# The wait for ScalarE's queue ahead of the centring of the expert weights, and the planner's margin for landings

## The chip, the cores and the metric

The kernel runs on one core of a Trainium2 chip (trn2). The metric is the device time of one execution in microseconds, lower is better; three executions of the kernel before gave 3122.73, 3131.1 and 3135.55 us, the median being 3131.1 us. Profiles come from one profiled execution of their own.

## The reference

Eight images of 256 channels and 32 by 32 pixels pass through two layers, all in float32.

- Layer 0: a group norm, then attention with 8 heads of 32 channels. Queries are a 1x1 product of the normed image. Keys and values come from another 1x1 product, averaged to four sizes (32, 16, 11 and 5 pixels a side, 1426 places in all), each with a depthwise 3x3 convolution added, then normed over channels. The heads' outputs are mixed by a small softmax matrix, projected and added to the image.
- Layer 1: the image is read as tokens. A layer norm and a single-head attention of size 256 over the image's 1024 tokens of 256 channels, added; a second layer norm, and a mixture of 8 experts, added.

The experts are what the change's weights belong to:

```python
feat = jnp.mean(x, axis=0)
w = jax.nn.softmax(feat @ Wr + br, axis=-1)
h = jnp.einsum('bfd,edh->bfeh', x, W1) + b1
h = jax.nn.relu(_bn(h, g1, be1, m1, v1))
h = jnp.einsum('bfeh,ehk->bfek', h, W2) + b2
h = jax.nn.relu(_bn(h, g2, be2, m2, v2))
y = jnp.einsum('bfeh,ehd->bfed', h, Wo) + bo
return jnp.einsum('bfed,fe->bfd', y, w)
```

The layer norm ahead of the experts subtracts the mean over channels. The kernel does that once in the weights instead of in each token: it multiplies each expert's W1 (and the router's Wr) by the matrix I - 1/256, which it calls `cm`, and stores the product as `w1c`.

## The kernel before

**Stages.** `attention` (L955) does layer 0 of all images and, beside it, layer 1 of the images that are through. `experts` (L2350) follows. A check at the end may send the program into a general version, which this data doesn't take.

**The main loop** (L2161 to L2206) runs over steps: for each image, each half of the channels (4 heads), each half of the pixels and 11 groups of up to 128 keys, plus one step per image for the last 25 keys of all halves: 45 steps an image, 360 in all. A step issues `scores` (L1651): four products of 32 x 512 into the one PSUM tile `sc`, and ScalarE's exponential of it into a tile `pt`; then `values` (L1661) of the step before, from `pt` into `pv`. Pairs of `pt` are added by GpSimd's accumulating DMA (`add`, L1706). As `sc` has one buffer, the scores of a step wait for the exponential of the one before.

**Threads.** All else is written as generators, each with a rank, that are spawned into a list (`spawn`, L883): keys and values of the next image, its depthwise convolutions on VectorE, pooling on GpSimd, the projection, layer 1 (`layer1`, `outputs`), and `weights1` (L1991). Each yields what it needs before its next instructions: an engine, tiles, and perhaps a PSUM tag; or a condition.

**The planner** is the class `Flow` (L666). While the program is built, every instruction issued through it is noted (`note`, L787): a cost by engine and size moves the engine's own clock `now`, and each tile gets a time at which it is ready. Each instruction is bound to follow the one issued before it on its engine, so the order in which the program is written is the order in which each engine works. After scores and after values the main loop calls `step` (L924), which resumes the first thread whose need is `runnable` (L897) until none is:

- A need of PE: a rank's credit (`PACE` and `PACE1` fill it each step), a free PSUM slot, and tiles landed, with `MARGIN`, before the time at which `sc` comes free.
- A need of another engine: if the tiles are there by that engine's clock, the engine may be ahead of TensorE by at most `AHEAD` (2.0 for ACT); else they have to land by TensorE's clock plus `NEAR`.
- `landed` (L893) is a tile's ready time, and `LATE` more if a DMA wrote it.

Where TensorE has a long planned wait and a PSUM slot is free, `warm` (L848) issues dummy products of constants.

**weights1** (L1991) runs after `mix` and ahead of `outputs` in one thread of rank 5 (L2145). It makes `cm`, the centred matrices of layer 1, and the folded batch norms; then, for each of the eight experts (L2059), loads W1 into `we` (SP's queue), yields a need of ACT with `we`, takes a second buffer of the same tag `res`, and runs `centred` (L1975): a need of PE with `src`, `cm` and a PSUM slot; four products of 128 x 256 (split in four of 32 columns each where TensorE works in that tiling); a need of ACT; ScalarE's copy to `wc`. SP stores `wc` to `w1c`. Then the router's weights follow in the same way, and `ready` lets `layer1` begin, once the first image's projection is done too.

**experts** begins when all images are projected. It loads the weights, then alternates first layers (`first7`) and second layers (`second`), while the rest of layer 1 runs as threads until `gates` has the router's weights (L2404, it needs the last image's layer 1). Up to there second layers are plain products (`half`, four of 512 columns) and their outputs go to memory; after it they use a seven-product form (`layer7`, `products`), and third layers are taken in between.

All instructions issued through the planner carry line L679 in the profile; groups are told apart by tile names.

Of the kernel before, what the change touches and what calls it, by code (L numbers as in the profile page):

```python
# [34 lines left out]
CAP = (1.5, 1.5)  # L35
NEVER = 1e9
MARGIN = 1.5
LATE = 3.0
AHEAD = {"DVE": 4.0, "ACT": 2.0, "POOL": 1.0, "SP": 10.0}
NEAR = {"DVE": 1.5, "ACT": 2.0, "POOL": 1.0, "SP": 10.0}  # L40
OWN = {"pt", "p1"}
# [624 lines left out]
class Flow:  # L666
# [226 lines left out]
    def landed(self, name):  # L893

        return self.ready.get(name, 0.0) + LATE * (self.writer.get(name) == "DMA")

# [58 lines left out]
def attention(tc, kit, f, outer, ended, nb, consts, x, t1, t2, hn, bounds, vecs, q_t, kv_t, proj_t, gqk_t, wqk, wqkv, vecs1, w1_d, w1c, gate_d, wrc, vecs2, bnvec, w2_d, h2d, between, pre, held):  # L955
# [6 lines left out]
    with ExitStack() as ctx:  # L962
# [5 lines left out]
        def T(pool, shape, tag, bufs=1):  # L968
            return f.tile(pool, shape, tag, bufs=bufs)

        def small():
            if f.also and f.free("sx") < min(map(f.end, f.slots.get("sm", [None]))):
                return T(psum, [P, 512], "sx")
            return T(shared, [P, 512], "sm", bufs=2)
# [57 lines left out]
        def rstd(out, var, eps, scale=1.0):  # L1032
            f.ve.tensor_scalar(out, var, scale, eps, ALU.mult, ALU.add)
            f.pool.tensor_tensor(out, out, kit.mhalf[: out.shape[0], 0:1].to_broadcast(out.shape), ALU.pow)
# [107 lines left out]
        def pe(*tiles, tag=None):  # L1142
            return "PE", tiles, tag

        def ve(*tiles):
            return "DVE", tiles, None

        def act(*tiles, tag=None):
            return "ACT", tiles, tag
# [825 lines left out]
        def centred(cm, src, width, dst):  # L1975

            yield pe(src, cm, tag="sm")
            ps = small()
            for m in range(2):
                for k in range(2):  # L1980
                    f.pe.matmul(
                        ps[:, m * width : (m + 1) * width],
                        lhsT=cm[:, k, m * P : (m + 1) * P],
                        rhs=src[:, k, :],
                        start=k == 0,
                        stop=k == 1,
                    )
            yield act(ps)
            f.act.activation(dst, ps[:, : 2 * width].rearrange("p (m f) -> p m f", m=2), AF.Copy)

        def weights1():  # L1991


            raw = T(l1, [P, 2, 512], "y")
            f.sp.dma_start(raw, wqk)
            wvr = T(l1, [P, 2, C], "p1", bufs=6)
            f.sp.dma_start(wvr, wqkv.rearrange("(k p) f -> p k f", p=P)[:, :, 2 * C :])
            cm = T(l1, [P, 2, C], "p1", bufs=6)
            bqkv = T(wp, [P, 6], "bqkv")
            f.sp.dma_start(bqkv, vecs1)  # L2000
            for k in range(2):
                for m in range(2):
                    f.ve.tensor_scalar(
                        cm[:, k, m * P : (m + 1) * P], ident, float(k == m), 1.0 / C, ALU.mult, ALU.subtract
                    )
            yield pe(raw, tag="sm")
            ps = small()
            for m in range(2):
                for k in range(2):
                    f.pe.matmul(  # L2010
                        ps[:, m * C : (m + 1) * C],
                        lhsT=raw[:, k, m * P : (m + 1) * P],
                        rhs=raw[:, k, C:],
                        start=k == 0,
                        stop=k == 1,
                    )
            yield ve(ps)
            g = T(l1, [P, 2, C], "p1", bufs=6)
            f.ve.tensor_copy(g, ps.rearrange("p (m f) -> p m f", m=2))
            yield from centred(cm, g, C, gw)  # L2020
            yield ve(gw)
            gm = T(wp, [P, 2], "gm")
            f.ve.tensor_reduce(gm, gw, AX.X, ALU.add)
            f.ve.tensor_scalar(gm, gm, 1.0 / C, None, ALU.mult)
            for k in range(2):
                f.ve.tensor_scalar(gw[:, k, :], gw[:, k, :], gm[:, k : k + 1], None, ALU.subtract)
            yield pe(bqkv, tag="sm")
            ps = small()
            for m in range(2):
                for k in range(2):  # L2030
                    f.pe.matmul(
                        ps[:, m : m + 1],
                        lhsT=raw[:, k, C + m * P : C + (m + 1) * P],
                        rhs=bqkv[:, k : k + 1],
                        start=k == 0,
                        stop=k == 1,
                    )
            yield ve(ps)
            u0 = T(wp, [P, 2, 1], "u0")
            f.ve.tensor_copy(u0, ps[:, 0:2].unsqueeze(2))  # L2040
            yield from centred(cm, u0, 1, gu.unsqueeze(2))
            yield from centred(cm, wvr, C, wv)
            f.ve.tensor_copy(gb, bqkv[:, 4:6])

            raw = T(l1, [P, 10, 2 * NE], "rec1")
            f.sp.dma_start(raw, vecs2)
            for i in range(2):
                b_, g_, be_, m_, v_ = (raw[:, 5 * i + u, :] for u in range(5))
                s = bnvec[:, (2 * i) * 2 * NE : (2 * i + 1) * 2 * NE]
                c = bnvec[:, (2 * i + 1) * 2 * NE : (2 * i + 2) * 2 * NE]  # L2050
                yield ve(raw)
                rstd(s, v_, 1e-3)
                yield ve(s)
                f.ve.tensor_tensor(s, s, g_, ALU.mult)
                f.ve.tensor_tensor(c, b_, m_, ALU.subtract)
                f.ve.tensor_tensor(c, c, s, ALU.mult)
                f.ve.tensor_tensor(c, c, be_, ALU.add)

            for e in range(NE):  # L2059
                we = T(l1, [P, 2, C], "res", bufs=2)  # L2060
                f.sp.dma_start(we, w1_d[:, e])
                yield act(we)
                wc = T(l1, [P, 2, C], "res", bufs=2)
                yield from centred(cm, we, C, wc)
                f.sp.dma_start(w1c[:, e], wc)
            wr = T(wp, [P, 2, NE], "wr")
            f.sp.dma_start(wr, gate_d[:, : 2 * NE].rearrange("p (k e) -> p k e", k=2))
            wrs = T(wp, [P, 2, NE], "wrs")
            yield from centred(cm, wr, NE, wrs)
            f.sp.dma_start(wrc, wrs)  # L2070
            f.drop(wvr, cm, g)
            ready.append(True)
# [70 lines left out]
        f.spawn(chain(*map(prepare, range(nb))), 4)  # L2143
        f.finish(lambda: key_parts[0] > 0)
        later.append(f.spawn(chain(mix(), weights1(), outputs()), 5))  # L2145
        f.spawn(layer1(), 6)
        aside = f.spawn(experts_ahead(), 8)
# [776 lines left out]
```

## Time and profile before

| what | us |
|---|---|
| median of three runs | 3131.1 |
| profiled execution, its own time | 3130.97 |
| its span, first to last instruction | 3128.8 |
| TensorE (PE) busy | 3034.8 |
| VectorE (DVE) busy | 2309.7 |
| ScalarE (ACT) busy | 1627.4 |
| GpSimd (POOL) busy | 1286.7 |
| TensorE's waits for ScalarE's exponential (sc <- ACT pt) | 39.3 |

The span is what the profile divides; 2.2 us lie around it. A line of a group gives engine, operation, output and inputs by tile names (numbers left out), shapes and count, and then times. Lines of waits give the total, how often, and the longest. A float32 product shows as two matmul records. The expert weights' loads run from 145.5 to 277.6 us of the span and the last store of a centred expert at 290.4 us; layer 1 begins with a load at 352.1 us, and the weights of the experts' stage are loaded from 1852.0 us on. The granted clock of TensorE is 0.993 in the mean.

### The profile page before, as it was taken

Reading aid. Unit: us, or ns where it says so; the run is one execution under the profiler, and the core shown is the slowest. Engines: PE = TensorE matmul, PEld = TensorE weight load, DVE = VectorE, ACT = ScalarE, POOL = GpSimd, SP = SyncE. Lnnn points to the kernel's source line nnn. Section 1 sums busy time; section 2 is a strip of 40 time slices with the busy share of each in tenths; the row PEclk is TensorE's granted clock in tenths of the full one; section 3 lists DMA queues with packets and bytes.
Section 4 is the critical chain, followed back from the end, with each engine's and each line's share of the span. In section 5 each row is a group of like instructions: output and inputs, shape, how many; then the busy total and the mean of one; then the engine's idle time right before and its main releaser. Section 6 shows DMA issues by size and latency. Waiting matters only on the chain.

```text
span 3128.8 us, 57003 instructions
## 1 busy us (share of the span) xinstructions
PE 3034.8 (97%) x23042; PEld 1781.0 (57%) x23042; DVE 2309.7 (74%) x3884; ACT 1627.4 (52%) x2176; POOL 1286.7 (41%) x1401
## 2 busy tenths in 40 slices
PE   7888999999999999999999999999999999999998
PEld 4323244343334343343433357778888888888887
DVE  6875988788977887788654444558888777777776
ACT  3776766666666666666655532343333344444443
POOL 3333432332242322322212120057655677777776
PEclk9999999999999999999999999999999999999999
DMA  1377766756756757656767663244443110000000
GB/s 56 83 151 169 159 134 135 167 125 132 171 108 143 173 112 148 152 125 145 171 148 156 125 204 125 105 169 143 143 152 135 46 37 25 31 21 21 21 14 22
DMA packets 113073, 360.24 MB, mean 115 GB/s; under 512 B 13776, under 2 KB 39928, under 8 KB 89344
## 3 DMA queue, kind: packets, MB, share of 16 engines
q0 software_dynamic: 28608, 181.68, 29.9%
q1 hardware_dynamic: 80688, 172.82, 16.3%
q8 instruction: 184, 3.01, 0.4%
q10 hardware_dynamic: 3504, 1.99, 0.2%
q14 instruction: 89, 0.73, 0.1%
HBM read 110.89 MB, written 78.16 MB: 60 GB/s over the span
## 4 chain that ended last, share of the span: by engine, by line
PE 74%; DVE 8%; issue 3%; ACT 2%; DMA 2%; POOL 2%; DVEq 0%; POOLq 0%; SPq 0%; ACTq 0%
PE bank L679 22%; PE sm L679 18%; PE y L679 11%; PE sc L679 8%; PE pv L679 8%; PE sx L679 7%; ACT pt L679 2%; DMA pt<-pt 1%; DVE acc L679 1%; DVE h L679 1%; DVE pt L679 1%; DVE sacc L679 1%; DVE u L679 1%; DVE c L679 1%; DMA hn<-pool 1%
## 5 line engine op out<-in xcount | busy, mean ns | idle before, releaser
L679 ACT ACTIVATE pt<-sc 128x2048 f32<-128x2048 f32 (+1 forms) x352 | 660.6, 1877 | 319.1 <-PE sc L679 238.8
L679 DVE TENSOR_TENSOR pt<-pt,pt 128x1024 f32<-128x1024 f32 x300 | 368.5, 1272 | 125.5 <-DMA pt<-pt 112.8
L679 PE MATMUL sc<-q,kn 32*128 32x512 f32 (+2 forms) x3072 | 417.0, 644 | 41.6 <-ACT pt L679 39.3
L679 PE MATMUL pv<-pt,vt 128*32 128x512 f32 (+1 forms) x2816 | 380.3, 612 | 0.0
L679 ACT ACTIVATE h<-h,bnvec 128x512 f32<-128x512 f32 x456 | 345.0, 805 | 62.6 <-DVE h L679 50.5
L679 ACT ACTIVATE p1c<-bank 128x256 f32<-128x256 f32 x228 | 87.1, 382 | 554.5 <-PE bank L679 554.3
L679 POOL TENSOR_TENSOR rstd<-rstd,mhalf 128x4 f32<-128x4 f32 (+1 forms) x96 | 116.1, 1210 | 609.4 <-DVE rstd L679 518.4
L679 DVE SCALAR_TENSOR_TENSOR acc<-map,vec,acc 128x961 f32<-128x961 f32 (+1 forms) x240 | 306.9, 1281 | 15.7 <-ACT acc L679 10.2
L679 DVE TENSOR_TENSOR h<-p1c,bank 128x512 f32<-128x512 f32 x228 | 155.2, 681 | 212.3 <-PE bank L679 209.1
L679 POOL DMA_DIRECT2D pt<-pt x160 | 147.0, 921 | 350.6 <-ACT pt L679 257.2
L679 POOL TENSOR_TENSOR tm<-h,tm 128x256 f32<-128x256 f32 x214 | 246.5, 1152 | 16.8
L679 DVE TENSOR_TENSOR h<-u,bank 128x256 f32<-128x256 f32 x456 | 232.0, 550 | 7.9
L679 PEld LDWEIGHTS sc<-q,kn 32*128 32x128 f32 (+2 forms) x3072 | 112.8, 177 | 209.0 <-ACT pt L679 93.6
L679 POOL TENSOR_TENSOR tm<-h 128x512 f32<-128x512 f32 x107 | 140.4, 1312 | 200.8 <-ACT h L679 200.8
L679 DVE SCALAR_TENSOR_TENSOR sacc<-small,vec,sacc 128x480 f32<-128x480 f32 (+8 forms) x384 | 201.7, 533 | 13.6 <-ACT sacc L679 3.6
L679 PEld LDWEIGHTS pv<-pt,vt 128*32 128x32 f32 (+1 forms) x2816 | 55.8, 108 | 271.9 <-issue 257.7
L679 DVE TENSOR_TENSOR h<-h,gate 128x1024 f32<-128x1024 f32 x128 | 203.9, 1593 | 0.5 <-ACT h L679 0.5
L679 PE MATMUL y<-t,s3e 128*128 128x256 f32 x768 | 187.0, 379 | 1.8 <-POOL t L679 1.8
L679 POOL TENSOR_TENSOR t<-h,t 128x256 f32<-128x256 f32 x220 | 175.4, 797 | 17.3
L679 POOL TENSOR_TENSOR t<-h 128x512 f32<-128x512 f32 x110 | 142.6, 1297 | 94.3 <-DVE h L679 79.9
L679 PE MATMUL bank<-t,s1e 128*128 128x256 f32 x726 | 177.2, 379 | 0.3 <-DVE h L679 0.2
L679 DVE TENSOR_TENSOR u<-h,bank 128x512 f32<-128x512 f32 x228 | 156.6, 687 | 24.2 <-PE bank L679 0.5
(369 smaller groups left out, 5619.7 us busy)
## 6 DMA issues: line engine op xcount, KB each, us to landing
pt<-pt POOLq DMA_DIRECT2D x160, 1024.0 KB, 7.8
h<-h SPq DMA_DIRECT2D x104, 512.0 KB
xi<-in_x_dram SPq DMA_DIRECT2D x16, 512.0 KB
t<-t SPq DMA_DIRECT2D x8, 1024.0 KB
res<-t SPq DMA_DIRECT2D x32, 256.0 KB
t<-res SPq DMA_DIRECT2D x32, 256.0 KB
hn<-res SPq DMA_DIRECT2D x32, 256.0 KB
hn<-hn SPq DMA_DIRECT2D x16, 512.0 KB
```

The lines of the kernel that those rows point to most:

```text
L679: ins = fn(*args, **kwargs)
```

## The change

The line that yields a need of ACT with the loaded weights is removed, so that the thread goes on at once to take the second buffer and to ask for TensorE; the load is then awaited there, as `src` in `centred`. And `LATE`, which `landed` adds to every tile written by a DMA, goes from 3.0 to 2.8, for the needs of all threads.

```diff
-LATE = 3.0
+LATE = 2.8
...
             for e in range(NE):
                 we = T(l1, [P, 2, C], "res", bufs=2)
                 f.sp.dma_start(we, w1_d[:, e])
-                yield act(we)
                 wc = T(l1, [P, 2, C], "res", bufs=2)
                 yield from centred(cm, we, C, wc)
                 f.sp.dma_start(w1c[:, e], wc)
```

No instruction of the computation is added or removed by the diff itself. As the planner's clocks depend on all that was issued before, both edits can alter the order of everything after the first load of an expert's weights.

## The prediction

> **What bounds the kernel now.** I read the page's header and slices first, then a table of stretches, then TensorE's waits, then the order in time around the change.
>
> ```profile
> span 3128.8 us, 57003 instructions
> PE 3034.8 (97%) x23042; PEld 1781.0 (57%) x23042; DVE 2309.7 (74%) x3884; ACT 1627.4 (52%) x2176; POOL 1286.7 (41%) x1401
> ```
>
> TensorE (PE) is busy in 97% of the span: 3128.8 - 3034.8 = 94 us are idle. The time is TensorE's work plus its idle time, so the question is whether the change alters either. The stretches say where the idle time lies (columns: length, then busy us of PE, its weight loads, VectorE, ScalarE, GpSimd; then granted clock, DMA share, GB/s):
>
> ```profile
> 0.00:100.00 100.00, 77.45 (x274) 38.71 (x274) 69.57 (x141) 48.08 (x88) 41.93 (x60) 0.97 0.20 60
> 100.00:420.00 320.00, 284.13 (x2463) 99.38 (x2462) 240.33 (x431) 214.09 (x260) 100.85 (x115) 0.97 0.67 146
> 420.00:1830.00 1410.00, 1394.01 (x14612) 568.62 (x14605) 1054.12 (x1913) 882.59 (x1036) 380.41 (x464) 1.00 0.66 143
> 1830.00:2040.00 210.00, 209.77 (x824) 149.45 (x823) 99.81 (x210) 65.97 (x110) 27.45 (x48) 0.99 0.40 141
> 2040.00:3129.00 1089.00, 1069.40 (x4881) 924.86 (x4879) 845.83 (x1193) 416.69 (x683) 736.10 (x715) 1.00 0.20 70
> ```
>
> Idle: 22.6 us at the start, 35.9 in the attention of image one and the start of two (100 to 420), 16.0 in the other images, 0.2 at the passage to the experts, 19.6 after it. The change acts in the second stretch; the reshuffle it sets off reaches the next two.
>
> ```profile
> PE sc L679 <- ACT pt L679: 39.3, 46, 2.6
> PE sx L679 <- DMA pt<-ptail: 2.9, 1, 2.9
> ```
>
> The largest wait is that of the scores for ScalarE's exponential of the step before; 24.8 us of it lie in 100 to 420. TensorE waited for a transfer once. How such a wait arises is seen in the order of time (start, length, what; in brackets idle time before it and its releaser):
>
> ```profile
> 274.51 1.93 PE L679 MATMUL sm<-res,p 128*32 128x256 f32 x32 [0.44 <-ACT bin L679]
> 279.52 1.14 PE L679 MATMUL sc<-q,kn 32*128 32x512 f32 x8 [1.00 <-ACT pt L679]
> 282.65 1.14 PE L679 MATMUL sc<-q,kn 32*128 32x512 f32 x8 [0.69 <-ACT pt L679]
> ```
>
> There is one score buffer, so scores, exponential and the next scores follow one another: 282.65 - 279.52 = 3.13 us at least. TensorE's own part of a step is 1.14 (scores) and 1.00 (the value products). A step into which the planner puts nothing else leaves 3.13 - 2.14 = 1.0 us idle, which is the wait shown at 279.52; one group of products (1.7 to 1.9 us) closes it. The expert weights' centring (sm<-res,p, 1.93) is such a filling.
>
> ```profile
> 180.60 0.33 SPq L679 DMA_DIRECT2D w1c<-res  x1
> 181.04 0.96 SPq L679 DMA_DIRECT2D res<-in_w_dram  x1
> 192.36 1.20 SPq L679 DMA_DIRECT2D res<-in_w_dram  x1
> ```
>
> One expert at a time: the load at 181.04 follows the store of the expert before by 0.44 us, its products run at 189.32, 8.3 us after the load. There is slack in that: eight experts take from 145.5 to 290.4.
>
> **What the Trainium skill says.** "TensorE: Matmul & The Clock Gate", the specification table at its head: ScalarE, VectorE and GpSimd take their queues strictly in order, and TensorE's reordering only pulls weight loads ahead of running matmuls. So a product helps only in the step where the planner wrote it. The trace agrees: TensorE stands for 1.00 us before scores although later products have their inputs. [...] the trace gives no landing time for the 256 KB weight loads, only the 8.3 us from load to use. "Perfetto Trace Analysis", Identifying the Most-Contended Engine: matmul busy time is no measure of nearness to the peak. I use it here only as the time that is not waiting, with the products' counts beside it.
>
> **The change, part by part.** Its size can't be read from the diff: the planner writes one order for the whole kernel, and both edits alter choices in it. I compared the orders of both builds, engine by engine, and priced them with durations of the trace. A step is one of the 360 groups of scores (45 per image); products are counted as the program issues them (the profile shows each f32 product twice).
>
> Removed wait. No instruction is removed: the eight loads, 8 x 1.9 = 15 us of products, eight copies of 0.60 us and eight stores remain. The place of the products moves. Before they follow steps 17, 20, 24, 27, 31, 37, 40 and 44, and the router's weights 47; after, 16, 22, 27, 30, 33, 39, 43, 48, and 51. So they do not come sooner: the first does, by one step, then the others spread, since the copy out of PSUM still asks for ScalarE and the product still asks for a landed load and a share of the step. That the set ends four steps later costs nothing: layer 1 needs also the first image's projection, which ends at step 57 or 58 in both orders, 6 steps (over 20 us) after. If that cover were gone, layer 1 would start some 4 x 4 us later (57 steps take about 250 us there), and other filling would be missing for that time.
>
> SP's queue. Loads and stores of weights change places with the pooled queries' stores (hn<-pool) and with an input copy (t<-in_x_dram). Each is 0.3 to 1.2 us of issue on a queue that is mostly empty, in steps whose filling doesn't read them: 0. Below nothing there is nothing to win either. If an expert's store stood waiting for its copy, the load of the next image (xi) would be behind it; in the new order that load stands ahead of the fifth store. 0, at most 2.
>
> Smaller margin. A product whose operand comes by DMA may be planned 0.2 us sooner. Were the transfer late each time, it would cost 0.2 us in each of about 100 places (8 loads of t, of xi, of the weights, the projection's inputs and products of them), 20 us; the trace shows one wait for a transfer, 2.9 us. At the other end a place taken 0.2 us sooner wins no more than a whole starved step now and then. I take 0; ends -3 and +5.
>
> The reshuffle: starved steps. For each step I sum what stands in it (scores 1.14, values 1.00, the rest by its rows; the planner's dummy products on constants left out) and take what is missing to 3.13. Before: 10.5 us in image one, 3.4 in image two, 2.8 in the six others, 16.7 in all, in 23 steps. After: 11.8, 5.5, 5.7, that is 23.0 in 27 steps. Steps with nothing at all beside scores and values rise from 12 to 23. Difference +6.3 us. The trace's waits for the exponential are 39.3 us where this sum gives 16.7, since ScalarE also has other work in front of it; in that proportion the difference would be 6.3 x 39.3 / 16.7 = 14.8. I take 6.3, as the waits of exactly 1.00 are the ones that the order decides; ends 0 and 15.
>
> The reshuffle: passage to the experts. Attention holds 1929 us of TensorE work after, 1960 before (the sums of all steps): two of the 32 layer-1 units (units 26 and 27, some 15 us each) now run among the experts' products. TensorE is full there (209.77 of 210.00), so this is moved, not saved. But the gates, which need the last image's layer 1, come later, and four more second layers run as plain products (16 of 512 columns) instead of the seven-product form (28 of 256). A plain one takes 8 x 0.465 = 3.72 us (55.8 us over 120 records), the other 3.02 (28 in 6.04 us in the chain's end), +0.70 each: +2.8 us. Twelve more intermediate tiles go out to memory and back, 24 transfers of 512 KB, where the DMA share is 0.42: 0, if that cover is gone perhaps 2. Dummy products fall from 13 units of 256 columns to 7, but they stand in idle time: 0, and in the sum above.
>
> Sum: +6.3 + 2.8 = +9 us. The profiled execution took 3130.97 us, 2.2 more than its span, and lies on the median of 3131.1. So 3131 + 9 = 3140 us, 0.3% slower, less than a measurement of this kernel tells from no change (0.5%, 15.6 us; the three runs before span 0.4%).
>
> **Rivals.** No difference (3131): the fewer dummies and starved steps trade places, because ScalarE, not the order, sets the waits; for it, that two thirds of the 39.3 us are not explained by my sum. Faster (3119): the products fill the waits of image one as the change intends. Half of its 24.8 us would be 12. Against it: of the seven steps from 29 to 45 that are empty in the old order, the weights come into just one (30), and the new order has others empty. Slower by over 0.5% (3156): each of the 11 further empty steps costs not 1.0 but up to the longest wait, 2.6 us, when the exponential stands behind copies or behind a GpSimd accumulation (pt<-pt, 7.8 us to landing) that ScalarE has to wait for; place: images one to eight; with 2.0 each it is 22 us, and with the 2.8 it gives 25. It decides from (15.6 - 2.8) / 11 = 1.2 us per empty step. That the change does nothing is excluded by the order.
>
> **Chances.** Forecast (+3 to +15) 0.45, no difference 0.27, faster 0.14, slower beyond 0.14. The range 3119 to 3156 reaches to both rivals' times; the likeliest case's own is 3134 to 3146. Faster by over 0.5% needs more than the fast rival's 12 us: 0.06. Slower by over 0.5%: 0.15. Within: 0.79.
>
> **What would show it.** Right: some 6 to 15 us more in the scores' wait for the exponential, spread over images two to eight too; 100 to 420 within 3 us of before; 144 records of 512-column products of w2e instead of 120; no new wait for a transfer. Wrong: a wait for landings of several us in TensorE's list (the margin), a shorter stretch to 420 (the fast rival), or single waits above 2 us at the empty steps (the slow one).

## The result and the profile after

The changed kernel took 3144.6 us (median of 10 runs, 3141.05 to 3149.64), the kernel before 3132.83 us in the runs beside it (10 runs). The ratio is 1.0041, 95% interval 1.0032 to 1.0049: 12.8 us slower, 10.0 to 15.4; the two medians alone differ by 11.8. The profiled execution of the changed kernel took 3145.04 us, with a span of 3143.2 us, 14.4 more than the span before.

The head of the page after:

```profile
span 3143.2 us, 56320 instructions
PE 3036.1 (97%) x22694; PEld 1782.1 (57%) x22694; DVE 2305.6 (73%) x3880; ACT 1625.5 (52%) x2172; POOL 1270.6 (40%) x1377
```

TensorE's busy time grew by 1.3 us; its idle time went from 94.0 to 107.1 us. Busy time holds the planner's dummy products too, 5.8 us before and 3.2 us after. Without them the work grew by 3.9 us (3029.0 to 3032.9) and the rest of the span by 10.5 us (99.8 to 110.3). So most of the loss is waiting. The same stretches as before, with the same columns (the first pair of numbers is the length and TensorE's busy time):

```profile
100.00:420.00 320.00, 286.54 (x2420) 99.44 (x2421) 241.25 (x437) 217.87 (x265) 99.28 (x118) 0.96 0.68 149
420.00:1830.00 1410.00, 1382.29 (x14287) 564.44 (x14286) 1047.31 (x1893) 878.00 (x1030) 389.27 (x462) 1.00 0.65 142
1830.00:2040.00 210.00, 209.31 (x820) 151.65 (x820) 98.43 (x213) 65.88 (x111) 30.56 (x50) 1.00 0.38 136
2040.00:3143.00 1103.00, 1080.78 (x4910) 928.53 (x4909) 849.68 (x1202) 417.23 (x684) 710.21 (x691) 0.99 0.24 82
```

From 100 to 420 us, where the edited code runs, idle time did not grow (33.5 us, before 35.9). It grew from 420 to 1830 us, from 16.0 to 27.7 us, long after the last expert weight was centred, and by 2.6 us after 2040. TensorE's waits after, whole execution (total, times, longest):

```profile
PE sc L679 <- ACT pt L679: 42.6, 49, 4.1
PE sx L679 <- issue: 3.5, 1, 3.5
PE sm L679 <- DMA t<-t: 2.3, 1, 2.3
```

The scores' wait for the exponential grew by 3.3 us. This total hides the wait that the prediction counted. For each wait of the scores I looked at what the exponential ahead of it had waited for. Where it had waited for its own scores alone, which is the bare chain of scores, exponential and scores, TensorE stood 20 times for 12.0 us before and 32 times for 20.7 us after. All other waits of the scores, behind ScalarE's other work, transfers or VectorE, fell from 28.4 to 22.4 us.

Two waits stand here that the kernel before did not have, and its one wait for a transfer (2.9 us for pt<-ptail) is gone. The second of the two, for the landing of an image of layer 1 (t<-t), has an entry of 2.3 us, 12 us after its transfer was issued. The first is at the passage to the experts. TensorE there (start, length, what, idle time before it):

```profile
1811.39 1.88 PE L679 MATMUL sm<-t,gw 128*128 128x512 f32 x4
1816.73 3.01 PE L679 MATMUL sx<-pt,con 128*32 128x512 f32 x8 [3.46 <-issue]
```

and VectorE, which makes the sum that this product reads:

```profile
1813.14 4.63 DVE L679 TENSOR_TENSOR pt<-pt,pt 128x1024 f32<-128x1024 f32 x4 [7.70 <-DMA pt<-pt]
```

VectorE waited 7.70 us for an accumulating transfer of GpSimd's queue, then added for 4.63 us, and the last unit's denominators could not start. The product then ran at half clock. In the order before, the same product followed without a wait of note (0.4 us idle between the last exponential and the experts' first load, against 4.1 after). TensorE had as much other work at this place in both orders: from the last value products to this sum it was busy for 5.75 us before and for 5.79 us after. What differs is the transfer. Before, with VectorE's sum, TensorE's product and the load of an image on SP's queue:

```profile
1806.72 0.86 POOL L679 DMA_DIRECT2D pt<-pt  x1 [7.80 <-ACT pt L679]
1814.30 2.36 DVE L679 TENSOR_TENSOR pt<-pt,pt 128x1024 f32<-128x1024 f32 x2 [1.78 <-DMA pt<-pt]
1818.57 2.14 PE L679 MATMUL sx<-pt,con 128*32 128x512 f32 x8
1818.77 0.43 SPq L679 DMA_DIRECT2D pt<-in_x_dram  x1
```

and after:

```profile
1800.56 0.40 SPq L679 DMA_DIRECT2D pt<-in_x_dram  x1
1800.80 0.87 POOL L679 DMA_DIRECT2D pt<-pt  x1 [6.67 <-ACT pt L679]
```

The transfer landed 7.48 us after its issue before, and 12.25 us after it in the changed kernel. There the load of 1 MB stands 0.24 us ahead of it; before, that load came 12 us behind it.

I divide each profile at the first and last exponential of the 360 steps (so that later tables can be compared). Idle time of TensorE, before and after: ahead of the steps 18.2 and 19.9; in the steps 56.0 and 60.6; to the experts' first load 0.4 and 4.1; to the gates 0.0 and 0.0; from the gates on 19.4 and 22.4. The sum of the differences is 13.0 us, beside the 1.3 us of busy time.

### The profile page after: what moved, and what is told of

Same layout as the page of the kernel before. It is cut to its first block, busy times and chain, and to the rows that moved or that the text cites. A ratio compares the mean times of both kernels' runs of the same rounds, so it can differ in the third digit from the quotient of the medians.

```text
span 3143.2 us, 56320 instructions
## 1 busy us (share of the span) xinstructions
PE 3036.1 (97%) x22694; PEld 1782.1 (57%) x22694; DVE 2305.6 (73%) x3880; ACT 1625.5 (52%) x2172; POOL 1270.6 (40%) x1377
## 3 DMA queue, kind: packets, MB, share of 16 engines
q0 software_dynamic: 28608, 181.68, 29.6%
q1 hardware_dynamic: 84144, 185.40, 17.4%
## 4 chain that ended last, share of the span: by engine, by line
PE 70%; DVE 9%; DMA 3%; issue 3%; ACT 2%; POOL 2%; DVEq 0%; POOLq 0%; ACTq 0%; SPq 0%
PE bank L679 22%; PE sm L679 16%; PE y L679 11%; PE sc L679 8%; PE pv L679 7%; PE sx L679 7%; DMA pt<-pt 2%; DVE pt L679 2%; ACT pt L679 2%; DVE acc L679 1%; DVE h L679 1%; DVE sacc L679 1%; DVE u L679 1%; DVE c L679 1%; POOL t L679 0%
## 5 line engine op out<-in xcount | busy, mean ns | idle before, releaser
L679 PE MATMUL sc<-q,kn 32*128 32x512 f32 (+2 forms) x3072 | 417.2, 644 | 43.7 <-ACT pt L679 42.6
L679 ACT ACTIVATE h<-h,bnvec 128x512 f32<-128x512 f32 x448 | 338.9, 805 | 63.8 <-DVE h L679 54.8
L679 DVE SCALAR_TENSOR_TENSOR acc<-map,vec,acc 128x961 f32<-128x961 f32 (+1 forms) x240 | 306.7, 1280 | 17.8 <-ACT acc L679 12.2
L679 POOL TENSOR_TENSOR tm<-h,tm 128x256 f32<-128x256 f32 x206 | 239.2, 1161 | 16.2
L679 PE MATMUL sm<-y,t 128*32 128x256 f32 (+1 forms) x1952 | 176.9, 380 | 1.2 <-DVE res L679 1.2
L679 POOL TENSOR_TENSOR t<-h,t 128x256 f32<-128x256 f32 x212 | 168.4, 794 | 16.6
```

What stands on the lines that cost most here:

```text
L679: ins = fn(*args, **kwargs)
```

## The experiments

All are compared with runs of the kernel before on the same chip. For each kernel with another order I counted, before it ran, the order's sum of starved steps as in the prediction; theory A is that the time follows this sum. The kernels are called e1 to e12.

**Each edit by itself.** Only the wait removed (e1):

```diff
-                yield act(we)
```

> Only the wait for ScalarE's queue is removed, the margin stays 3.0. Theory A (the time follows the order's sum of starved steps, plus 0.70 us for each second layer that runs plain instead of in seven products): the order's sum is 23.8 us against 16.4 before, and one more plain second layer (20 against 19), so 7.4 + 0.7 = +8 us, ratio about 1.0026. Rival B (the smaller margin lets TensorE reach tiles before they land, and that is what costs): no cost here, ratio 1.000, no wait for a transfer in TensorE's list. Rival C (any other order costs or wins by accidents that the sum does not see): anything within +-0.5%, not ordered by the sum over the four kernels of this set.

Measured: 3152.83 us, ratio 1.0068 (1.0049 to 1.0087). Only the margin (e2):

```diff
-LATE = 3.0
+LATE = 2.8
```

> Only the margin for landings goes to 2.8, the wait for ScalarE's queue stays. Theory A: the order's sum of starved steps is 23.3 us against 16.4, one more plain second layer, so 6.9 + 0.7 = +8 us, ratio about 1.0024, although dummies rise from 13 to 19 units. Rival B: this carries the whole loss, ratio about 1.004, with waits for transfers of 2 us and more in TensorE's list. Rival C: within +-0.5%, not ordered by the sum.

Measured: 3146.77 us, ratio 1.0047 (1.0033 to 1.0060). Theory A has the sign of both and the size of neither: it expected 8 us for each, and some 21 and 15 us were lost. Each edit alone loses more than, or as much as, both together (1.0041), so the effects of the two do not add up: each makes another order. Rival B does not hold: the removed wait alone, with the margin as before, costs most, and neither profile shows a wait for a transfer after 420 us.

**Two more orders.** The wait removed and a margin of 3.4 (e3):

```diff
-LATE = 3.0
+LATE = 3.4
...
-                yield act(we)
```

> The wait for ScalarE's queue removed, the margin larger, 3.4. Theory A: the order has fewer starved steps than before (11 empty steps, sum 14.0 against 16.4) and two more plain second layers (21 against 19), so -2.4 + 1.4 = -1 us, ratio about 1.000 (0.9985 to 1.001). Rival B: a larger margin can only take waits for landings away, of which there was one of 2.9 us: ratio 0.999 to 1.000 as well. Rival C: within +-0.5%, not ordered by the sum.

Measured: 3144.03 us, ratio 1.0038 (1.0024 to 1.0052). Theory A missed this one. The scores' wait did fall, to 31.0 us, as the sum of 14.0 says, and the idle time in the steps was that of before (56.4 us). But other waits took the place, which the sum doesn't hold: 6.3 us for VectorE's sums of pairs, 4.2 of them at the passage, where TensorE stood for 5.1 us in all; 3.8 us for the copy of a value bank; and, in spite of the larger margin, 4.2 us for loads of expert weights (res<-in_w_dram). Rival B, by which a larger margin only takes such waits away, misses here too. The wait kept and a margin of 2.7 (e4):

```diff
-LATE = 3.0
+LATE = 2.7
```

> The wait for ScalarE's queue stays, the margin is 2.7. Theory A: the sum of starved steps is 29.6 us, the largest of the orders looked at, one more plain second layer: 13.2 + 0.7 = +14 us, ratio about 1.0044. Rival B: a margin smaller still than 2.8 costs more than that one, with waits for transfers in TensorE's list. Rival C: within +-0.5%, not ordered by the sum. If A holds, the four ratios stand in the order e3, then e1 and e2, then e4.

Measured: 3168.67 us, ratio 1.0119 (1.0099 to 1.0139). The four ratios stand in the order that theory A foretold, e3, then e2 and e1, then e4, and two of them lie beyond rival C's 0.5%. The scores' wait is 60.4 us. But the loss is over twice the 14 us expected, as in e1 and nearly in e2. In e4 TensorE has no wait for a transfer of over 0.8 us, against rival B.

**A larger margin that should lose, a smaller one that should not.** Rival B is tried at its opposite ends. The wait kept and a margin of 3.05 (e5):

```diff
-LATE = 3.0
+LATE = 3.05
```

> The kernel before with a slightly larger margin for landings, 3.05 instead of 3.0; the wait for ScalarE's queue stays. Theory A (starved steps of the order): its sum is 32.9 us against 16.4, 28 empty steps against 12, one more plain second layer. The four runs so far gave 1.3 us of TensorE idle time in the steps per us of the sum, so +21 us there, and about 10 us that all of them had outside; +25 to +40 us, ratio 1.008 to 1.013. Rival B (a smaller margin costs by waits for landings, a larger one can't): ratio 1.000. Rival C (accidents of the order that the sum doesn't see): 0.998 to 1.008.

Measured: 3165.27 us, ratio 1.0103 (1.0086 to 1.0120). A margin larger by 0.05 us in the planner's reckoning costs 32 us. That is inside what was expected, but this expectation had been fitted to the four runs above, to 1.3 us of idle time in the steps for each us of the sum and 10 us besides. And the removed wait with a margin of 2.6 (e6):

```diff
-LATE = 3.0
+LATE = 2.6
...
-                yield act(we)
```

> The wait for ScalarE's queue removed, the margin 2.6, smaller than in the change. Theory A: the sum of starved steps is 16.1 us against 16.4 before, with as many plain second layers (19): 0 from these two terms; with what all four reordered kernels had outside the steps, 0 to +10 us, ratio 1.000 to 1.003, that is less than the change as made. Rival B: a margin still smaller than 2.8 costs more than the change, ratio above 1.0045. Rival C: anything within +-0.8%.

Measured: 3130.8 us, ratio 0.9995 (0.9985 to 1.0006), no loss, so the 10 us besides do not belong to every changed order. Its scores' wait, beside that of the kernel with 3.05, first this one:

```profile
PE sc L679 <- ACT pt L679: 34.3, 38, 4.2
```

then the one with 3.05:

```profile
PE sc L679 <- ACT pt L679: 48.5, 57, 3.2
```

The eight orders side by side, by the sum of starved steps:

| kernel | sum in the order, us | waits of the bare chain, us | TensorE idle in the steps, us | ratio |
|---|---|---|---|---|
| e3 | 14.0 | 9.8 | 56.4 | 1.0038 |
| e6 | 16.1 | 14.4 | 53.1 | 0.9995 |
| before | 16.4 | 12.0 | 56.0 | 1 |
| changed | 22.8 | 20.7 | 60.6 | 1.0041 |
| e2 | 23.3 | 16.3 | 62.4 | 1.0047 |
| e1 | 23.8 | 16.6 | 68.5 | 1.0068 |
| e4 | 29.6 | 20.5 | 74.7 | 1.0119 |
| e5 | 32.9 | 24.5 | 73.4 | 1.0103 |

The sums of the kernel before and of the changed one are counted anew here; the prediction had 16.7 and 23.0. A straight line through the sum and the idle time gives 1.15 us of idle time in the steps for each us of the sum, and 1.4 us where the dummies count as idle, as they do in the sum. Through the sum and the waits of the bare chain it gives 0.7 us. So the price taken per starved step, its bare 1.0 us, is near for TensorE's idle time, and neither edit has a price of its own: what they do to the order has. The time rises faster. The ratios rise with the sum, save e3, and save e5, which lies below e4 (their intervals overlap); a straight line through them gives 1.8 us of time for each us of the sum and misses e3 by 11 us. e4 and e5 lost 37 and 32 us, with 18.7 and 17.4 us more idle time in the steps.

**The dummies.** The changed kernel, its order kept (e7), with each dummy noted by the planner as before but issued with one column:

```diff
-            self.pe.matmul(t[:, :C], lhsT=self.kit.ones, rhs=self.kit.con[:, :C], start=True, stop=True)
+            ones, con = self.kit.ones, self.kit.con[:, :C]
+            cuts = range(0, P, DH) if self.narrow(ones, con) else (None,)
+            for j in cuts:
+                s = slice(None) if j is None else slice(j, j + DH)
+                ins = self.tc.nc.tensor.matmul(t[s, :1], lhsT=ones[:, s], rhs=con[:, :1], start=True, stop=True)
+                self.note("PE", "matmul", ins, (t[s, :C],), {"lhsT": ones[:, s], "rhs": con})
```

> The changed kernel with its order kept, and each planned dummy product (seven units of 256 columns in all) cut to one column, so that TensorE does nothing in these places. Theory A: the dummies stand in idle time, so the time is that of the changed kernel, ratio 1.003 to 1.005 against the kernel before. Rival: the dummies are work on the path, then 7 x 0.48 = 3 us less, ratio 1.002 to 1.004; or they keep the granted clock up, then it is slower than the changed kernel.

Measured: 3146.61 us, ratio 1.0042 (1.0026 to 1.0058), that of the changed kernel. TensorE's idle time in the steps rose from 60.6 to 67.3 us, and the time stayed. The dummies stand in idle time, as the prediction took it.

**Plain second layers.** The kernel before, 18 more of them plain (e8):

```diff
+            if i % 6 == 0:
+                tms.pop(i, None)
             if i in tms:
```

> The kernel before, its attention untouched, with 18 more of the experts' second layers as plain products of 512 columns instead of the seven-product form (37 against 19). Prediction's step: 0.70 us each, 18 x 0.70 = +12.6 us, ratio 1.0040. Rival: the plain form also spares sums on VectorE and combinations that TensorE waits for (6.8 us of waits for VectorE in that stage), so less than half of it, +0 to +6 us, ratio 1.000 to 1.002.

Measured: 3140.6 us, ratio 1.0017 (1.0007 to 1.0026), 5.3 us or 0.3 us for each (0.12 to 0.45). The prediction's 0.70 was over twice too large. From the gates on the span grew by 6.7 us (1087.5 to 1094.2) and TensorE's busy time by 6.5 us. Its idle time there stayed (19.4 and 19.5 us): the waits for VectorE's sums fell from 6.8 to 5.7 us, and others grew as much. So the rival has the size but not the cause. The price itself was mis-sized. One plain layer at full clock, seen in the changed kernel, and the product after it:

```profile
2055.76 3.60 PE L679 MATMUL bank<-h,w2e 128*128 128x512 f32 x8
2059.20 1.03 PE L679 MATMUL bank<-hn,w1e 128*128 128x256 f32 x4
```

It holds TensorE for 2059.20 - 2055.76 = 3.44 us, 0.42 us more than the 3.02 of the other form. The mean of 0.465 us, from which the prediction took 3.72, also held the time by which each group overlaps the next (3.60 shown, 3.44 to the next start) and layers at half clock, such as this one in the kernel before:

```profile
2030.79 5.38 PE L679 MATMUL bank<-h,w2e 128*128 128x512 f32 x8
```

**The kernel before again, and filled steps.** While reading the changed kernel I saw its products run at half their speed after a cluster of starved steps:

```profile
283.47 1.14 PE L679 MATMUL sc<-q,kn 32*121 32x512 f32 x8 [1.00 <-ACT pt L679]
284.53 1.06 PE L679 MATMUL pv<-pt,vt 128*32 128x512 f32 x8
288.78 2.09 PE L679 MATMUL sc<-q,kn 32*128 32x512 f32 x8 [3.18 <-ACT pt L679]
290.80 1.93 PE L679 MATMUL pv<-pt,vt 121*32 121x512 f32 x8
292.66 1.93 PE L679 MATMUL pv<-ptail,vz 32*32 32x512 f32 x8
294.52 2.09 PE L679 MATMUL sc<-q,kn 32*128 32x512 f32 x8
```

The table of stretches shows that the granted clock had fallen (it is the third last column):

```profile
285.00:290.00 5.00, 1.82 (x16) 0.51 (x8) 2.73 (x2) 1.88 (x1) 4.69 (x7) 0.79 0.84 231
290.00:295.00 5.00, 5.00 (x26) 0.88 (x24) 0.00 (x0) 2.22 (x2) 3.77 (x6) 0.50 0.95 195
```

The exponential ahead of the wait of 3.18 us was late for another reason than a starved step. It had stood for GpSimd's accumulating transfer:

```profile
286.85 1.88 ACT L679 ACTIVATE pt<-sc 121x2048 f32<-121x2048 f32 x1 [3.44 <-DMA pt<-pt]
```

Windows at half clock might still make a starved step dearer than its 1.0 us, and explain the steep rise of the ratios. So I tried a theory A': put dummies where TensorE stands, and the windows go, and time with them. First a control (e9):

> The kernel before, unchanged, as a control of what one profile says. Ratio 1.000. If the start of the profile (about 1.5 us more idle time ahead of the first step in nearly all the other kernels) and the wait at the passage belong to the run and not to the order, they are seen here too: idle time before the first step about 20 us instead of 18.2, the rest of the idle time within 3 us of the first profile. If they belong to the order, they are as in the first profile of this kernel.

Measured: 3132.48 us, ratio 1.0004 (0.9995 to 1.0014). Idle time 18.7 us ahead of the steps, 54.1 in them, 1.3 at the passage. So a profile repeats to about 2 us in a stretch, and of the 1.7 us more ahead of the steps in the changed kernel part is such scatter. Then the filled steps, in the changed kernel (e10), the kernel before (e11) and e6 (e12), each with its order otherwise unchanged:

```diff
+                placed = f.last["PE"]
                 f.step((PACE, PACE1))
+                if f.last["PE"] == placed and f.free("sm") <= f.now["PE"]:
+                    f.occupy()
...
+    def occupy(self):
+
+        bank, self.keep = self.keep, None
+        t = bank()
+        self.open.discard(t.name)
+        for j in range(0, P, DH):
+            ins = self.tc.nc.tensor.matmul(
+                t[j : j + DH, :384], lhsT=self.kit.ones[:, j : j + DH], rhs=self.kit.con[:, :384], start=True, stop=True
+            )
...
+            self.last["PE"] = ins.ins.name
+        self.keep = bank
```

> The changed kernel with its order kept, and in each step in which the planner placed no product, one extra group of dummy products of 384 columns (0.75 us) in the 1.0 us that TensorE would stand. Theory A' (a starved step costs its 1.0 us of waiting, and a cluster of them besides halves the granted clock for 3.4 us or more, as at 289 to 297 us, which doubles the time of the products there): the waits stay, the half-clock windows after the first step fall from 10 to 6 or fewer, 4 to 8 us less than the changed kernel: ratio against the kernel before 1.0015 to 1.003. Rival (the clock plays no part, the step's own wait is all): as the changed kernel, 1.0041, or slower by what the dummies delay the next scores (25 x 0.1 us = 2 us).

> The kernel before with the same extra dummy products in the steps without a product (about half as many as in the changed kernel). Theory A': 2 to 4 us less, ratio 0.9988 to 0.9995, fewer half-clock windows after the first step than the 9 of before. Rival: 1.000 to 1.0005.

> The wait for ScalarE's queue removed, margin 2.6, which gave 0.9995, with the same extra dummy products. Theory A': 2 to 4 us less than without them, ratio 0.998 to 0.999, the fastest of all kernels here. Rival: 0.9995 or 1.000.

Measured: the changed kernel filled 3144.15 us, 1.0032 (1.0020 to 1.0044); the kernel before filled 3132.45 us, 0.9997 (0.9989 to 1.0005); the kernel with margin 2.6 filled 3132.54 us, 0.9999 (0.9991 to 1.0007). In the changed kernel the scores' wait fell from 42.6 us to this:

```profile
PE sc L679 <- ACT pt L679: 31.0, 47, 5.0
```

and all idle time from 107.1 to 95.3 us, near that of the kernel before, while the time hardly moved. Theory A' falls: it asked for 4 to 8 us here (0.9 thousandths, some 3 us, were seen, inside both intervals) and for 2 to 4 us in the other two, which gained nothing. In the stretches at half clock that began after 90 us, without the last one at the end of the run, TensorE spent 30.7 us in the kernel before and 30.7 us in the changed one, so this can't be the difference. It was 23.9 us in both of them when filled, but also in the control, where nothing was filled. Around the first step, at 86 us, half clock lasted 3.4 us in the first profile of the kernel before and 10.2 us in the second, as in the changed kernel. Only e5 had clearly more from 90 us on, 44.4 us. The filled steps show something else besides: what a starved step lacks is not work for TensorE, for its length is that of the chain through ScalarE. Keeping TensorE busy in it changes the table, not the time.

## Why the prediction was right, point by point

The forecast, 3140 us, is 4.6 us below the measured median, and the difference of +9 us lies below the measured 10.0 to 15.4. The sign and the main mechanism were right. That the size came so near is in part luck, as the last paragraphs of this section say.

- *The products do not come sooner.* Right. The last store of a centred expert comes at 306.8 us instead of 290.4. Idle time from 100 to 420 us is within 3 us of before, as the prediction asked. The second image ended 6.2 us earlier than in the first profile of the kernel before, but 2.0 us earlier than in the second (504.1, 510.3, 506.1 us). No kernel with the wait removed was measurably faster than before (e1, e3, e6, the change).
- *SP's queue, the end of weights1 four steps later: 0.* Layer 1 began with its load at 353.6 us, before at 352.1, though the weights were done 16 us later. The new order of SP's queue was not tried by itself. One move on it, of which the prediction did not speak, may have cost something at the passage (below).
- *The smaller margin: 0, ends -3 and +5.* Right as to the wait for landings: one new wait of 2.3 us, and the old one of 2.9 us gone. The kernel with only the smaller margin has none and still loses 0.47%. The margin acts through the order. What the step passed over is that 0.05 us of it can reorder the kernel and cost 32 us.
- *Starved steps: +6.3 us.* Right in mechanism and, within what profiles scatter, in size. The waits of the bare chain grew from 12.0 us (13.6 in the control) to 20.7 (19.2 in e7, which has the same order). The idle time in the steps, dummies counted as idle, went from 61.8 us (59.9) to 63.8 (67.6), so by 2 to 8 us. The place was half right: the prediction had over half of the growth in images one and two, where idle time did not grow; all of it lies in the six others. The proportion with the scores' whole wait (14.8 us) would have been too much. The sign to look for, 6 to 15 us more in the scores' wait alone, did not show in that total, which grew by 3.3 us, as waits of other kinds fell.
- *Passage to the experts.* The moved units are there: the experts' weights load at 1833.7 us instead of 1852.0, the gates' store comes at 2076.2 instead of 2041.3, and 144 records of plain 512-column products of w2e stand for 120. The price of +2.8 us is too high: 4 x 0.3 = 1.2 us by the test, 4 x 0.42 = 1.7 by the trace. (The DMA share that the prediction sets beside it, 0.42, is 0.40 in its own table.) What it left out is a wait of 3.5 us: the last accumulating transfer landed 12.25 us after its issue instead of 7.48. The 1 MB load that the new order sets just ahead of it may be why. In e10, which has the same order, that load came 1.25 us behind the transfer, which landed after 9.14 us, and TensorE waited 1.6 us; but in the control, with no such load near, it also took 9.04 us, and in e4 and e5, beside other transfers, 12.2 and 11.4 us with that load 3.9 and 5.2 us behind. No run isolates it.
- *Dummies: 0.* Right (1.0042 against 1.0041).
- *The slow rival*, up to 2.6 us per further empty step, did not come about as a sum: all of the measured loss over its 11 steps would be 12.8 / 11 = 1.2 us each, and part of it lies elsewhere. But its sign, single waits above 2 us, was seen. The changed kernel has four such waits of the scores, 12.8 us together, the longest 4.1; the kernel before has three of 7.5 us, and four of 9.4 in the control. Two of the four, those at 288.78 and 1078.00 us, stand behind GpSimd's accumulating transfer, as that rival said.

Two profiles of each order, in us; e7 differs from the changed kernel by its dummies alone, which count as idle here:

| where | before, and control (e9) | changed, and e7 |
|---|---|---|
| idle ahead of the steps | 18.2, 18.7 | 19.9, 20.0 |
| idle in the steps | 61.8, 59.9 | 63.8, 67.6 |
| idle to the experts' first load | 0.4, 1.3 | 4.1, 4.1 |
| idle from the gates on | 19.4, 19.1 | 22.4, 22.9 |
| work | 3029.0, 3028.6 | 3032.9, 3030.5 |

In the mean that is 1.5, 4.9, 3.3, 3.4 and 2.9 us, 16 in all between these profiles. The prediction had a price for the steps and, inside the work, for the plain layers: 9 us, of which some 6 to 7 were found there. The rest of the loss lies in places that it put at nothing: the passage, the time from the gates on and the start. Terms left out made up for a price too high.

The four orders e1 to e4, priced in the same way, show how much of the nearness is luck: 8, 8, -1 and 14 us were expected, and 21, 15, 12 and 37 us were lost.

Open: why the time rises by about 1.8 us for each us of the sum where the idle time in the steps rises by 1.15. For e4 and e5 part of it is the profile taken: e4's was its fastest run (3160.18 us, 8.5 below its median), e5's its slowest (3170.16, 4.9 above). In e5's profile TensorE is also busy 13.6 us longer, of which its 13.7 us more at half clock can explain half.

## What to carry to other kernels

Where a planner writes the order of a whole kernel, an edit of one wait or one margin has no price of its own; build both, compare the orders, and price what differs. Here the sum of what each step lacks to the length of its chain ordered eight kernels by TensorE's idle time in the steps, to within 4 us of a straight line fitted to them; for the time it gave most of their ranking, and not the size. When work is moved, ask also which transfers now run beside each other, and take a price from instructions at full clock, not from a mean that mixes clocks. And a constant in such a planner (3.0 here) suits one order only: 3.05 was 1% worse, so it should be tried again after each edit, with enough runs to see 0.3%.

## What the runs showed of the hardware

The granted clock of TensorE fell to one half without a wholly idle stretch of 3.4 us. In the changed kernel it fell at 287.85 us; in the 3.41 us ahead of that TensorE was busy for 1.16 us, and its longest wait there lasted 3.18 us. For 10.24 us the products then took about twice as long, 2.09 and 1.93 us in place of 1.14 and 1.06. At 1041.8 us of the kernel before it fell after 1.55 us of busy time in 3.41 us, with a longest wait of 1.83 us. The Trainium skill, "TensorE: Matmul & The Clock Gate", Part 1, states half rate after an idle window of about 3.4 us; the waits here were shorter. The clock also fell after a stretch that the profile counts as busy throughout: in the kernel before, the router's 32 product records of 8 columns each fill 2027.30 to 2030.93 us, and from 2031.65 us the granted clock was 0.5 for 3.41 us.
